# A graph layer on one core: 71 single rows a step in three register loads, one more filler, and the second block's gather places computed first

## The chip, the cores and the metric

The kernel runs on one core of a Trainium2 chip. The metric is the device time of one execution in microseconds (us), as the median of the runs; lower is better. The engines are named as the profile names them: PE multiplies matrices, PEld loads its weights, DVE is the vector engine, ACT the scalar engine, POOL issues the indirect gathers, SP is the sync engine. SP and ACT also issue direct DMAs; that work is not counted as busy time of an engine and shows as SPq and ACTq.

## The reference

There are 50,000 nodes with 128 numbers each, and 1,650,000 directed edges sorted by their destination. Every node has one edge to itself, and it is the last of the edges to that node.

```python
msg = where(edge_type == 0, x[src] @ W_data.T + b_data, x[src] @ W_control.T + b_control)
agg = segment_sum(msg, dst, 50000)
out = relu(agg + x @ W_self.T + b_self)
result = layernorm(x + out)          # over the 128 numbers of a node
```

## The kernel before

The kernel sums the rows of x first and multiplies by the weights once for each block of nodes.

**Blocks and steps.** The edge list is cut into NBLK blocks of Q = 2 steps. Block 0 and the last block are plain: they hold gathered edges alone, and the last one takes what is left. In every other block a step has 1,536 + F + S edges. R = 12 columns of 128 edges (SIZES) are fetched by 12 indirect gathers on POOL, so a full block has 24 gathers. S edges are single rows: each is fetched by a direct DMA of its own, 512 bytes, TURNS[0] of them from SP and TURNS[1] from ACT. F edges are fillers. Their rows come in place of self edges among the 1,536: a self edge need not be gathered, since the node's own column of x is added from x_t. `fill` puts the fillers' indices in the first F places of self edges that it finds in the step; if any step has fewer than F self edges among its 1,536, the program sets a flag in `find_bad` (through `loops`) and a second, general path runs. With the numbers before, F = 42 and S = 64, a block has 3,284 edges, NBLK is 503, and the last block has 13 gathers.

**Passes.** `gathers` issues 6 indirect gathers (PASS) for a tile y of which there are 10 (SLOTS); a tile is free again when PE has used it. So POOL can be 60 gathers ahead of PE. `products` multiplies each gathered column by a one-hot matrix `oh` of the destinations and adds it up in PSUM. In the last pass of a step the single rows come as one more product: PE first waits in `rows_fetched` until all the single rows of the block have landed.

**DVE.** For each block DVE computes the one-hot matrix of the block two ahead (`onehot`, `counts`, AHEAD = 2), and the gather indices of the block five ahead (`fill`, RAHEAD = 5), besides the sums, the moments and the normalised rows of earlier blocks (`add`, `begin_sums`, `moments`, `store`).

**Single rows.** `offsets` turns the source indices of a block into byte offsets on DVE, three blocks ahead. `single_rows(b, part)` loads a part of these offsets into registers, one load instruction (line 476) on SP and one on ACT, and then issues one DMA for each register (line 481). Before the change there are two parts of 32 registers on each engine. In the main loop the parts of block b + 2 stand in passes 0 and 1 of block b. Their tile `yx` has four buffers, so a buffer is free when PE is done with the block four before. On ACT the square root of every second block (`root`, line 583) stands behind the single rows, on SP the load of x's columns (`window`, line 421), the edge lists of the next ten blocks (`load_edges`, `spread_out`, `spread_in`) and the store of a block (`store_rows`, line 597). Each engine does what it has in the order of the program.

**Start.** Block 0's gathers need nothing but the first index tile. Block 1's gathers wait for `fill(1)`. Before the change DVE first does `positions(0)`, `onehot(0)` and `counts(0)`, and then `fill(1)`. PE has, ahead of its first product, the small products of `left_out_columns(1)` to `left_out_columns(4)`, each of which waits for that block's `fill`.

Of the kernel before, what the change touches and what calls it, by code (L numbers as in the profile page):

```python
# [37 lines left out]
PASS = 6  # L38
B = 112
C = R * Q  # L40
F = 42
TURNS = (32, 32)
S = sum(TURNS)
LOADS = 2
BEGIN = (0, -(-Q * TURNS[0] // 4) * 4)
X = BEGIN[1] + -(-Q * TURNS[1] // 4) * 4
R1 = R + 1
# [3 lines left out]
CE = Q * SIZE  # L51
BE = CE + Q * (F + S)
NBLK = 2 + (E - CE) // BE
# [33 lines left out]
def plain(b):  # L87

    return b == 0 or b >= NBLK - 1
# [6 lines left out]
def straight(ctx, tc, c, x, x_t, edges_t, edges_f, src_x, dst_first, first_p, out):  # L96
# [35 lines left out]
                   allow_small_or_imprecise_dtypes=True)  # L132
    FILL = Q * F + C1
    small = keep_ps.tile([P, 2 * W + F + 2 * FILL + 2], F32, name="small")
    num_ps, rank_no_ps = small[:, :2 * W], small[:, 2 * W:2 * W + F]
    lists = [small[:, 2 * W + F + i * FILL:][:, :FILL] for i in range(2)]
    sums_at = [small[:Q * F, 2 * W + F + 2 * FILL + i:][:, :1] for i in range(2)]

# [85 lines left out]
    def clear_sums():  # L224
        for t in sums:
            nc.vector.memset(t, 0.0)
            nc.vector.memset(t[0:3, 2, :], 1.0)
            nc.vector.memset(t[0:2, 2, :], 0.0)
# [122 lines left out]
    def left_out_columns(b):  # L351

        if not plain(b):
            pc = sums_at[b % 2]
            nc.tensor.matmul(pc, bys.pop(b).rearrange("p q f -> p (q f)"), ones_b[:, 0:1], start=True, stop=True)
            pcs[b] = pc

    def left_out_matrix(b):
        if not plain(b):
            z = fil.tile([Q * F, 2, P], BF16, name="z", bufs=RAHEAD + 1)  # L360
            at = fil.tile([Q * F, 1], F32, name="at")
            nc.vector.tensor_copy(at, pcs.pop(b))
            nc.vector.tensor_scalar(z.rearrange("p t n -> p (t n)"), node_no, at, None, op0=ALU.is_equal)
            zs[b] = z
# [44 lines left out]
    def window(b):  # L409
        if b % SPAN:  # L410
            return
        n = min(SPAN, NBLK - b)
        w = b // SPAN
        _, regs = nc.values_load_multi_w_load_instructions(
            base_i[0:1, w, :1 + n], engines=[SP], min_val=0, max_val=(N - B) * ROW,
            skip_runtime_bounds_check_because=CLAMPED)
        for i in range(n):
            bases[b + i] = regs[1 + i]
        at = nc.s_assert_within(regs[0], 0, (N - WIDE) * 4, skip_runtime_bounds_check_because=CLAMPED)
        xw = stp.tile([P, WIDE], F32, name="xw")  # L420
        nc.sync.dma_start(xw.bitcast(U8), x_t_bytes[:, bass.ds(at, 4 * WIDE)])
        wides[w] = xw

    def positions(b):

        _, regs = nc.values_load_multi_w_load_instructions(
            at_i[0:1, b, :], engines=[DVE], min_val=0, max_val=WIDE - B, skip_runtime_bounds_check_because=CLAMPED)
        tops = [B - W] * Q + [B, WIDE - B]
        places[b] = [nc.s_assert_within(r, 0, top, skip_runtime_bounds_check_because=CLAMPED)
                     for r, top in zip(regs, tops)]  # L430
        xT = stp.tile([P, B], F32, name="xT", bufs=5)
        nc.vector.tensor_copy(xT, wides[b // SPAN][:, bass.ds(places[b][3], B)])  # L432
        xTs[b] = xT

    def onehot(b):
        g, i = divmod(b, GB)
        oh = ohp.tile([P, C1, 2 * W], F32, name="oh")
        nc.vector.tensor_tensor(oh, col_g[g][:, i, :, None].to_broadcast([P, C1, 2 * W]),  # L438
                                num_ps[:, None, :].to_broadcast([P, C1, 2 * W]), op=ALU.is_equal)
        ohs[b] = oh  # L440

    def counts(b):

        cnt = ohp.tile([P, Q, 2 * W], BF16, name="cnt")
        with nc.allow_low_precision(reason="whole numbers up to R1"):
            nc.vector.tensor_reduce(cnt, ohs[b].rearrange("p (q r) w -> p q w r", r=R1), AX.X, ALU.add)  # L446
        cnts[b] = cnt
# [14 lines left out]

    def part_of(n, part):

        return min(n, 32 * part)

    def single_rows(b, part):

        if part == 0:
            ys[b] = stp.tile([S, Q, D], F32, name="yx", bufs=ROW_SLOTS)  # L470
        both = []
        for j, (eng, dma) in enumerate(((SP, nc.sync), (ACT, nc.scalar))):
            n = Q * TURNS[j]
            k0, k1 = part_of(n, part), part_of(n, part + 1)
            at = BEGIN[j]
            _, rows = nc.values_load_multi_w_load_instructions(ats[b][0:1, at + k0:at + k1], engines=[eng], **RANGE)
            both.append([(dma, fetched[j][b % ROW_SLOTS], *divmod(k0 + k, TURNS[j]), sum(TURNS[:j]), row)
                         for k, row in enumerate(rows)])
        for pair in zip_longest(*both):
            for dma, sem, q, k, at, row in filter(None, pair):  # L480
                copy = dma.dma_start(ys[b][at + k:at + k + 1, q, :].bitcast(U8), x_bytes[:, bass.ds(row, ROW)])
                copy.then_inc(sem, 16)
                tc.no_tile_sem_insts.add(copy.ins.name)
                tc.add_to_no_dep_group(f"single{b}", copy.ins)

    def rows_fetched(b):

        times = len(range(b % ROW_SLOTS or ROW_SLOTS, b + 1, ROW_SLOTS))
        for j in range(2):
            wait = nc.tensor.wait_ge(fetched[j][b % ROW_SLOTS], 16 * Q * TURNS[j] * times)  # L490
        tc.declare_fence(wait.ins, group=f"single{b}")
# [85 lines left out]
    def pair(b):  # L577

        return range(b // 2 * 2, b + 1) if b % 2 == 1 or b == NBLK - 1 else ()
# [55 lines left out]
    spread_out(0)  # L635
    spread_in(0)
    window(0)
    positions(0)
    onehot(0)
    counts(0)  # L640
    for b in range(1, RAHEAD):
        fill(b)
        left_out_columns(b)
        left_out_matrix(b)
        if b < AHEAD:
            onehot(b)
            counts(b)
            for part in range(LOADS):
                single_rows(b, part)
        if b == 1:  # L650
            clear_sums()
    ready = []
    for b in range(NBLK + 1):
# [20 lines left out]
        for q, (step, ks) in enumerate(passes_of(b)):  # L674
# [20 lines left out]
            if q == 1 and b > 1 and pair(b - 2):  # L695
                store(pair(b - 2))
                ready.extend(pair(b - 2))
            if q < LOADS and not plain(b + AHEAD):
                single_rows(b + AHEAD, q)
# [231 lines left out]
def gnn_resnorm(  # L931
# [46 lines left out]
    with ExitStack() as own:  # L978
        straight(own, tc, c, x, x_t, edges_t, edges_f, src_x, dst_first, first_p, out)
# [60 lines left out]
```

## Time and profile before

| | us |
|---|---|
| median of 3 runs | 15131.09 |
| lowest and highest run | 15127.51, 15135.05 |
| the profiled execution | 15137.27 |
| its span, first to last instruction | 15135.5 |
| POOL busy in it | 11419.4 (75%) |
| DVE busy in it | 10825.4 (72%) |
| PE busy in it | 7996.4 (53%) |

The span is 1.8 us shorter than the execution's own time. A timeline row has the start, the length, the engine, the line, what it does and how often, and in brackets how long the engine had been idle before and what ended that. Equal instructions of an engine that follow each other are merged in one row with their count: the length then goes from the start of the first to the end of the last. DMA issues on SP and ACT are such rows too. A row of a line (line 476, say) has the shortest, the median and the longest of its instructions in ns.

### The profile page before, as it was taken

What the parts mean: (1) busy time and instruction counts of PE and PEld (TensorE: products, weight loads), DVE (VectorE), ACT (ScalarE), POOL (GpSimd) and SP (SyncE); (2) the same over time, 40 slices, a digit from 0 to 9 for tenths busy, and PEclk for the clock granted to TensorE, in tenths of its full rate; (3) what the DMA queues carried; (4) which work ended last, traced back from release to release, by engine and by line L of the source; (5) the groups of instructions that cost most, each with busy time, mean ns of one, the idle gap of its engine ahead of it and who ended that gap; (6) DMA issues with size and microseconds to landing.
All of it is one profiled execution on the core that took longest, in us unless ns stands there. A gap on an engine that the chain in (4) does not pass through costs nothing. (4 is left out here: it accounts for less than half of the span.)

```text
span 15135.5 us, 239743 instructions
## 1 busy us (share of the span) xinstructions
PE 7996.4 (53%) x35339; PEld 6888.2 (46%) x35340; DVE 10825.4 (72%) x14081; ACT 77.8 (1%) x258; POOL 11419.4 (75%) x12071
## 2 busy tenths in 40 slices
PE   3555555555555555555555555555555555555555
PEld 3444444444444444444444444444444444444444
DVE  8777777776777777777777777777777777777775
ACT  0000000000000000000000000000000000000000
POOL 7777777777777777777777777777777777777777
PEclk7555555555555555555555555555555555555555
DMA  2222222222222222222222222222222222222222
GB/s 64 63 62 62 63 63 61 63 62 63 62 63 63 62 62 63 63 62 62 63 63 62 62 63 63 62 62 63 63 62 62 63 63 62 63 62 63 62 63 57
DMA packets 616955, 941.51 MB, mean 62 GB/s; under 512 B 272160, under 2 KB 409151, under 8 KB 615358
## 3 DMA queue, kind: packets, MB, share of 16 engines
q0 software_dynamic: 385968, 791.19, 21.8%
q1 hardware_dynamic: 164824, 118.13, 3.2%
q10 hardware_dynamic: 64566, 16.74, 0.8%
q14 instruction: 1309, 10.72, 0.2%
q8 instruction: 288, 4.72, 0.1%
HBM read 895.97 MB, written 29.02 MB: 61 GB/s over the span
## 5 line engine op out<-in xcount | busy, mean ns | idle before, releaser
L507 POOL DMA_INDIRECT y<-in_x,idx x12048 | 11405.6, 947 | 3690.8 <-issue 3598.2
L526 PE MATMUL acc<-oh,y 128*128 128x120 f32 x24122 | 5724.9, 426 | 6958.6 <-PEq L514 6911.9
L526 PEld LDWEIGHTS acc<-oh,y 128*128 128x128 f32 x24122 | 5178.2, 323 | 7419.1 <-PEq L514 7365.9
L540 DVE TENSOR_TENSOR sums<-acc,sums 128x180 f32 x1006 | 340.1, 338 | 3743.3 <-PE acc L535 3676.7
L446 DVE TENSOR_REDUCE cnt<-oh 128x240 bf16<-128x3120 f32 x503 | 2927.9, 5821 | 17.5
L438 DVE TENSOR_TENSOR oh<-col,small 128x3120 f32<-128x3120 f32 x503 | 1702.6, 3385 | 0.0
L348 DVE TENSOR_REDUCE by<-old 128x84 bf16<-128x1092 f32 x501 | 1067.5, 2131 | 17.4
L532 PE MATMUL acc<-oh,yx 64*128 64x120 f32 x2004 | 764.1, 482 | 0.0
L329 DVE TENSOR_TENSOR m<-rk,small 128x1092 f32<-128x1092 f32 x501 | 647.0, 1291 | 17.1
L332 DVE TENSOR_TENSOR new<-m,small 128x1092 f32<-128x1092 f32 x501 | 646.9, 1291 | 17.0
L336 DVE TENSOR_REDUCE v_new<-new 128x26 f32<-128x1092 f32 x501 | 646.6, 1291 | 17.0
L345 DVE TENSOR_TENSOR old<-m,small 128x1092 f32<-128x1092 f32 x501 | 642.8, 1283 | 0.0
L532 PEld LDWEIGHTS acc<-oh,yx 64*128 64x128 f32 x2004 | 488.6, 303 | 206.2 <-issue 200.0
L561 PE MATMUL po<-wmsgT,sums 128*112 128x128 f32 x2012 | 528.9, 409 | 0.0
L561 PEld LDWEIGHTS po<-wmsgT,sums 128*112 128x112 f32 x2012 | 384.6, 262 | 108.6 <-issue 89.7
L559 PE MATMUL po<-bias,sums 3*112 3x128 f32 x1006 | 341.7, 435 | 0.0
L558 PE MATMUL po<-wselfT,xT 128*112 128x128 f32 x1006 | 293.6, 391 | 0.0
L535 PE MATMUL acc<-cnt,to_row 128*128 128x60 bf16 x2012 | 278.1, 228 | 0.0
L551 DVE TENSOR_TENSOR sums<-pl,sums 128x336 f32<-128x336 f32 x501 | 254.0, 507 | 17.3
L558 PEld LDWEIGHTS po<-wselfT,xT 128*112 128x112 f32 x1006 | 257.4, 302 | 0.0
L559 PEld LDWEIGHTS po<-bias,sums 3*112 3x112 f32 x1006 | 197.8, 249 | 112.2 <-issue 96.6
L380 DVE TENSOR_TENSOR pl<-pl,xT 128x224 f32<-128x224 f32 x501 | 199.9, 399 | 53.5 <-DVE xT L432 2.1
(129 smaller groups left out, 3601.6 us busy)
## 6 DMA issues: line engine op xcount, KB each, us to landing
yx<-in_x ACTq DMA_DIRECT2D x32064, 0.5 KB
yx<-in_x SPq DMA_DIRECT2D x32064, 0.5 KB
y<-in_x,idx POOLq DMA_INDIRECT x12048
xw<-in_x_t SPq DMA_DIRECT2D x126, 224.0 KB
out<-o SPq DMA_DIRECT2D x503, 56.0 KB
vf_all<-vd SPq DMA_DIRECT2D x51, 420.0 KB
sdt<-in_edges_t SPq DMA_DIRECT2D x51, 390.0 KB
one_g<-in_src_x SPq DMA_DIRECT2D x51, 5.0 KB
```

Source lines behind the costliest of these rows:

```text
L329: nc.vector.tensor_tensor(m, rk_g[g][:, i, :, None].to_broadcast([P, C1, F]), rank_no_ps[:, None, :].to_broadcast([P, C1, F]), op=ALU.is_e ...
L332: nc.vector.tensor_tensor(new.rearrange("p (q r) f -> p q r f", r=R1), m.rearrange("p (q r) f -> p q r f", r=R1), vf.rearrange("p (q f) -> ...
L336: nc.vector.tensor_reduce(v, new, AX.X, ALU.add)
L345: nc.vector.tensor_tensor(old, m, cb[:, :, None].to_broadcast([P, C1, F]), op=ALU.mult)
L348: nc.vector.tensor_reduce(by, old.rearrange("p (q r) f -> p q f r", r=R1), AX.X, ALU.add)
L438: nc.vector.tensor_tensor(oh, col_g[g][:, i, :, None].to_broadcast([P, C1, 2 * W]), num_ps[:, None, :].to_broadcast([P, C1, 2 * W]), op=AL ...
L446: nc.vector.tensor_reduce(cnt, ohs[b].rearrange("p (q r) w -> p q w r", r=R1), AX.X, ALU.add)
L507: copy = nc.gpsimd.indirect_dma_start(out=y[:r, k % PASS, :].bitcast(U8), out_offset=None, in_=x_rows, in_offset=bass.IndirectOffsetOnAxis ...
L526: nc.tensor.matmul(acc[:, :2, :].rearrange("p t w -> p (t w)"), y[:r, k % PASS, :], ohs[b][:r, column(k), :], start=k == of_step[0], stop= ...
L532: nc.tensor.matmul(acc[:, :2, :].rearrange("p t w -> p (t w)"), ys[b][:, q, :], ohs[b][:S, q * R1 + R, :], start=False, stop=True)
L558: nc.tensor.matmul(po, xT, c["wselfT"], start=True, stop=False)
L561: nc.tensor.matmul(po, a[:, t, :B], c["wmsgT"][:, t * D:(t + 1) * D], start=False, stop=t == 1)
```

## The change

F goes from 42 to 43, TURNS from (32, 32) to (35, 36), so S from 64 to 71, and LOADS from 2 to 3. `part_of` cuts a block's rows on an engine into three parts at multiples of four: SP has 70 rows for a block, loaded as 24, 24 and 22 registers, and ACT has 72, loaded as 24, 24 and 24. The third part stands in pass 2. A full block then has 3,300 edges instead of 3,284, still with 24 gathers; NBLK becomes 501 instead of 503, and the last block is left with 228 edges, so 2 gathers. In the start, `positions(0)`, `onehot(0)` and `counts(0)` move behind `fill(1)` and what follows it for block 1.

```diff
-F = 42
-TURNS = (32, 32)
+F = 43
+TURNS = (35, 36)
 S = sum(TURNS)
-LOADS = 2
+LOADS = 3
...
     def part_of(n, part):
 
-        return min(n, 32 * part)
+        return -(-n * part // (4 * LOADS)) * 4 if part < LOADS else n
...
     window(0)
-    positions(0)
-    onehot(0)
-    counts(0)
     for b in range(1, RAHEAD):
         fill(b)
         left_out_columns(b)
         left_out_matrix(b)
+        if b == 1:
+            positions(0)
+            onehot(0)
+            counts(0)
         if b < AHEAD:
             onehot(b)
             counts(b)
```

## Prediction

> **What bounds the kernel now.** I read the page's costliest groups first, then the waits, then POOL's busy time in two long windows.
>
> ```profile
> L507 POOL DMA_INDIRECT y<-in_x,idx x12048 | 11405.6, 947 | 3690.8 <-issue 3598.2
> L526 PE MATMUL acc<-oh,y 128*128 128x120 f32 x24122 | 5724.9, 426 | 6958.6 <-PEq L514 6911.9
> L348 DVE TENSOR_REDUCE by<-old 128x84 bf16<-128x1092 f32 x501 | 1067.5, 2131 | 17.4
> L532 PE MATMUL acc<-oh,yx 64*128 64x120 f32 x2004 | 764.1, 482 | 0.0
> L329 DVE TENSOR_TENSOR m<-rk,small 128x1092 f32<-128x1092 f32 x501 | 647.0, 1291 | 17.1
> ```
>
> ```profile
> POOL y L507 <- issue: 3601.5, 11798, 0.3
> POOL y L507 <- PE acc L526: 28.5, 84, 3.2
> DVE sums L540 <- PE acc L535: 3676.7, 457, 14.3
> ```
>
> ```profile
> 3000.00:9000.00 6000.00, 4536.90 (x4794) 0.55 0.26 62
> 9000.00:15000.00 6000.00, 4536.22 (x4796) 0.53 0.26 62
> ```
>
> POOL is busy only 75% of the span, but its gaps are of one kind: 11,798 gaps of at most 0.3 us, put down to issue, which means that nothing the profile shows held it back. With 4,795 gathers in 6,000 us a gather comes every 1.2513 us, in both windows. PE's idle time is waiting in its queue (PEq) at line 514, which is the wait for gathered rows, and DVE's is waiting for PE. So the gathers set the pace: 24 of them give 30.03 us per block.
>
> **The gathers.** Before the last block there were 502 blocks of 24, so 12,048 gathers; now there are 500 of 24, 12,000. That is 48 x 1.2513 = 60.1 us less. The rest of the change only matters where it keeps POOL from this pace.
>
> **The end.** The last block drops from 13 gathers to 2.
>
> ```profile
> 15097.48 0.94 POOL L507 DMA_INDIRECT y<-in_x,idx  x1 [0.30 <-issue]
> ...
> 15105.03 0.35 DVE L540 TENSOR_TENSOR sums<-acc,sums 128x180 f32 x1
> ...
> 15118.80 0.76 PE L559 MATMUL po<-bias,sums 3*112 3x128 f32 x2
> ```
>
> The last full block's last gather starts at 15097.48, its sums are there at 15105.38. The products of its layer, which need these sums, run only at 15118.80, behind the passes of the last 13 gathers. With two gathers, which start 2.5 us after 15097.48, nothing stands between. 11 gathers are 13.8 us of POOL, and the layer can come 13.4 us earlier at most; a part of DVE's work on the last block gets in the way. I take 12.5 (bounds 0, if the tail were one fixed chain, and 13.8).
>
> **The start.** Here the change looks better than it is.
>
> ```profile
> 25.79 0.35 SPq L316 DMA_DIRECT2D vf_all<-vd  x1
> 27.14 0.38 SPq L421 DMA_DIRECT2D xw<-in_x_t  x1
> ```
>
> ```profile
> 31.40 0.22 DVE L432 COPY xT<-xw 128x112 f32 x1 [5.13 <-DMA xw<-in_x_t]
> ...
> 40.66 0.24 DVE L326 COPY small<-vf_all 128x84 f32<-128x84 f32 x1
> ```
>
> ```profile
> 45.80 0.94 POOL L507 DMA_INDIRECT y<-in_x,idx  x1 [9.52 <-DVE idx L340]
> ```
>
> ```profile
> 90.35 0.23 PE L355 MATMUL small<-ones_b,by 128*84 128x1 bf16 x1 [9.12 <-DVE by L348]
> ...
> 93.64 0.94 POOL L507 DMA_INDIRECT y<-in_x,idx  x1 [3.17 <-PE acc L526]
> ```
>
> POOL waits 9.52 us for block 1's indices, because `fill(1)` starts at 40.66 behind the one-hot work of block 0. Moved ahead, the indices come about 9 us earlier and this wait goes. What is late next is the row at 93.64: the 61st gather needs the first tile of ten back, and PE begins only after the small product at 90.35, which waits for the `fill` of block 4. Those fills lie at the end of the same DVE work, in another order. So POOL reaches gather 61 nine us earlier and waits there some 11 us instead of 3.17. What remains is a shorter start of DVE: it no longer waits for xw until 31.40 but for vf_all, which was issued 1.35 us earlier on the same queue; against it, four fills are longer by 26 of 1092 elements in each of five operations, (4 x 1.29 + 2.13) x 0.024 = 0.17 us each, 0.7 in all. When vf_all lands no row shows, only that it was there at 40.66. I take 0.7 us of gain, between a loss of 5 and a gain of 9.5 (if the slots did not bind).
>
> **Fillers and wider tiles elsewhere.** The 0.17 us per block on DVE lie under its 3676.7 us of waiting for PE, 7.3 us per block. A single-row product has 71 rows of weights instead of 64; one with 128 takes 426 ns and one with 64 takes 482, so rows cost nothing.
>
> **The single rows.** This is the part that can go wrong. SP and ACT issue the DMAs one by one, and both have more to do per block.
>
> ```profile
> 7523.21 10.36 ACTq L481 DMA_DIRECT2D yx<-in_x  x32
> ```
>
> ```profile
> 7523.21 23.51 ACTq L481 DMA_DIRECT2D yx<-in_x  x64
> 7555.61 0.29 ACT L583 ACTIVATE sd<-mv,eps 112x2 f32<-112x2 f32 x1 [60.67 <-DVE at L362]
> 7557.97 49.45 ACTq L481 DMA_DIRECT2D yx<-in_x  x128
> 7615.74 0.30 ACT L583 ACTIVATE sd<-mv,eps 112x2 f32<-112x2 f32 x1 [59.83 <-DVE at L362]
> ```
>
> ```profile
> L476 SPq TENSOR_LOAD <-at_x x799: 1864/2120/2358, 2999.3 to 14988.5; - x200
> L476 ACTq TENSOR_LOAD <-at_x x799: 2131/2233/2457, 3001.3 to 14983.1; - x200
> ```
>
> ```profile
> L980 ACTq TENSOR_LOAD <-bad x1: 463/463/463, 15125.4 to 15125.4; - x1
> ...
> L980 SPq TENSOR_LOAD <-bad x1: 482/482/482, 15130.0 to 15130.0; - x1
> ```
>
> On ACT, 32 DMAs take 10.36 us, so one every (10.36 - 0.23) / 31 = 0.327, a DMA's own 0.23 at the end. The difference between 128 and 64 rows, 49.45 - 23.51 = 25.94 us, is one block: two stretches of 10.36 and two load gaps of 2.61, of which the load is 2.23. Between the end of the second row and the square root at 7615.74 ACT is idle for 8 us in two blocks. A load of one register takes 0.463 and one of 32 takes 2.233: 0.057 per register and 0.41 fixed, so 1.78 for 24. The new block on ACT is three parts of 10.36 - 8 x 0.327 = 7.74 for the DMAs, 1.78 for the load and 0.38 of the gap around it: 29.7 us. By the four parts of the third row, (49.45 + 2.61) / 4 = 13.0 each, it is 29.9. I take 29.8, against 30.03 that the gathers take. So ACT fits, with 0.2 us left of 4.
>
> The Trainium skill, page "DMA: Bandwidth & Descriptors", section "Latency and other measured facts", puts a floor of about 600 ns under a register load. By that floor a load of 24 is 1.83 and the block on ACT an estimated 29.95 us, just under the gathers' pace; the trace's load of one register, at 0.463, is below the floor, so I keep 29.8.
>
> SP has 70 rows, and other work.
>
> ```profile
> 7530.75 23.29 SPq L481 DMA_DIRECT2D yx<-in_x  x64
> 7554.20 0.34 SPq L597 DMA_DIRECT2D out<-o  x1
> 7556.81 23.18 SPq L481 DMA_DIRECT2D yx<-in_x  x64
> ```
>
> From 7530.75 to 7556.81 is a block with its store and without waiting: 26.06. Six rows more are 2.0, six registers more 0.3, the third load's fixed part and gap 0.6: 29.0. A window every fourth block and the lists every tenth add about 0.5 on average, an estimate from the lengths of such rows (0.38, 0.35) and of a load. 29.5 is under 30.03 too.
>
> Neither margin has to hold in every block. The rows of a block are issued two blocks ahead, so ACT can fall some 55 us behind before PE waits, and PE some 60 us behind before POOL finds no free tile (60 gathers, 75 us, less the pass being worked on). Part of this reserve is used early:
>
> ```profile
> 501.38 41.45 ACTq L481 DMA_DIRECT2D yx<-in_x  x96
> ```
>
> Three parts take 41.45 us here, where they later take 49.45 - 12.97 = 36.5. If that is typical of the first 900 us, ACT loses 2 to 4 us a block there, 40 to 80 us, and wins it back at 0.2 us a block. I expect PE to lag POOL by tens of us in the first third, at no cost to POOL.
>
> **The sum.** 60.1 + 12.5 + 0.7 = 73.3 us less. The profiled execution took 15137.27 (span 15135.5 and 1.8 around it), so it would take 15064; the median of the runs is 6.2 below the profiled one, which gives 15058 us.
>
> **Rivals.**
>
> *ACT's queue becomes the bound (slower).* The mechanism: the third load costs more than its 24 registers suggest, or the DMAs come at 0.34 instead of 0.327, and a block on ACT takes longer than 30.03. For it speaks how thin the margin is; 0.013 us on each of 72 DMAs is 0.9 us a block. Against it, all loads and DMAs of the later windows are alike, and the sum by two rows is 29.7 and 29.9. If the block takes W, 499 blocks fall 499 x (W - 30.03) behind; the reserve of some 60 us takes the first 0.12. From W = 30.15 on the gain shrinks, and from 30.3 on it is gone. At 30.5 the cost is 235 - 60 = 175, so about 15230 us. The far end is a load of 24 that costs what one of 32 does, 2.23: then W is 31.2, the cost 520 and the time 15580.
>
> *It comes out even.* The same with W at 30.2 to 30.3, so 25 to 75 us of the 73 are lost: 15083 to 15133, most of it within 0.2% of before.
>
> *The start gives its full 9.5 us.* If PE's first products did not wait for the fills, POOL would gain the whole wait at 45.80: 15049. The row at 90.35 speaks against it.
>
> *The change doesn't do what it says.* With 43 fillers a step needs 43 self edges among its 1,536, or the general path runs, which would take far longer. The inputs decide this, not the trace: a count over the sorted edges finds the fewest in any step to be exactly 43, so it is enough.
>
> *Register loads priced per register.* At a price that made three loads of 24 dearer than the DMAs they feed, ACT would be bound in any case: with 0.2 us per register W is 3 x (7.74 + 4.8 + 0.38) = 38.8 us and the time about 19400. The 2.233 us for 32 registers are 0.07 each, so no chance is left for it. The Trainium skill states that figure, about 200 ns a register even in bulk, on the page "Runtime: NRT & Kernel Launch", section "Instruction fetch mechanics", for loads from HBM; the trace's loads, from a tile, do not follow it.
>
> **How the numbers follow.** The forecast has 0.68, the full start 0.03, ACT as the bound 0.20, the even case 0.09, the last two nothing. A change of 0.2% (30 us) is about what a measurement of this kernel can tell from none. Faster by more than that: 0.71; within it: 0.09; slower: 0.20. The forecast's own range is 15045 (full start, full tail) to 15085 (5 us lost at the start, no gain at the end, ACT slightly over). The range reaches on to 15165, through the even case and the beginning of the slower one.
>
> **What would show it.** Right: 12,002 gathers, still 1.251 us apart; ACT's square root hardly idle, with the rows of a block some 29.8 us apart; a register load of 24 at 1.78; DVE waiting for the square root in early blocks; at the start no wait of POOL for indices and one of about 11 us for the 61st gather. Wrong: POOL waiting for PE in hundreds of gathers with blocks more than 30.1 us apart and ACT never idle, a load of 24 above 1.9, or POOL's pitch itself longer than 1.2513.

## The result and the profile after

The changed kernel took 15452.74 us, the median of 6 runs (15449.53 to 15453.82). The kernel before took 15128.06 on the same chip (6 runs, 15124.21 to 15135.05). The ratio is 1.0213, with an interval of 1.02 to 1.0227: the change costs 2.1%. Forecast were 15058 and a range from 15045 to 15165. The profiled execution has a span of 15451.7 us; what follows is read from it.

The chain that ended last, on the page of the changed kernel, by engine and then by line:

```profile
ACTq 68%; issue 16%; DVE 12%; DMA 2%; PE 1%; POOL 1%; ACT 0%; SPq 0%; DVEq 0%; PEldq 0%; POOLq 0%
ACTq L481 56%; ACTq L476 12%; DVE cnt L446 3%; DVE oh L438 2%; DMA yx<-in_x 1%; DVE sums L540 1%; DVE o L592 1%; POOL y L507 1%; DVE m L329 1%; DVE new L332 1%; DVE v_new L336 1%; DVE old L345 0%; PE acc L526 0%; ACT sd L583 0%; DVE rstd L589 0%
```

More than two thirds of the span go through ACT's queue: the row DMAs of line 481 and their register loads of line 476. The gathers on POOL, which set the pace before, have 1%. The waits and the costliest groups of the changed kernel say the same:

```profile
ACT sd L583 <- issue: 15071.0, 246, 63.5
PE acc L532 <- PEq L490: 4535.9, 448, 21.9
POOL y L507 <- issue: 3503.9, 11477, 0.3
DVE rstd L589 <- ACT sd L583: 2635.5, 246, 12.4
POOL y L507 <- PE acc L526: 234.5, 127, 10.9
POOL y L507 <- PE acc L532: 197.4, 31, 10.6
```

```profile
L507 POOL DMA_INDIRECT y<-in_x,idx x12000 | 11333.9, 944 | 4049.1 <-issue 3503.3 <-PE acc L526 234.5 <-PE acc L532 197.4
L532 PE MATMUL acc<-oh,yx 71*128 71x120 f32 x1996 | 584.0, 386 | 4536.1 <-PEq L490 4535.9
L348 DVE TENSOR_REDUCE by<-old 128x86 bf16<-128x1118 f32 x499 | 1083.4, 2171 | 17.2
```

PE now waits at line 490, for single rows, 448 times in 499 blocks; before, the idle time ahead of the row product was 0.0. ACT's square root, once in two blocks, stands behind nothing but rows: 15071.0 / 246 = 61.26 us of idle time and 0.29 of its own make 61.55 us for two blocks, 30.78 for one. The gathers need 30.03, so POOL now waits for PE. Its busy time fell by 71.7 us and its idle time rose by 358.3 (4049.1 against 3690.8).

POOL's busy time in the two windows of the changed kernel:

```profile
3000.00:9000.00 6000.00, 4411.13 (x4673) 0.61 0.29 61
9000.00:15000.00 6000.00, 4408.35 (x4670) 0.61 0.29 61
```

A gather now comes every 1.284 us instead of 1.2513.

Why ACT's block got longer is not in the loads. The register loads of the changed kernel from 3 to 15 ms, and two blocks of ACT's queue:

```profile
L476 ACTq TENSOR_LOAD <-at_x x1168: 1658/1774/2038, 3007.5 to 14999.9; - x195
```

```profile
12000.97 59.91 ACTq L481 DMA_DIRECT2D yx<-in_x  x144
12060.98 0.29 ACT L583 ACTIVATE sd<-mv,eps 112x2 f32<-112x2 f32 x1 [61.62 <-issue]
```

The load of 24 takes 1.774, as forecast. ACT issues 144 rows in 59.91 us with no pause but the loads, and within a part its DMAs are 0.349 us apart on average, not 0.327. What lengthens them shows where a block of rows ends. The timeline of the changed kernel:

```profile
7994.25 60.54 ACTq L481 DMA_DIRECT2D yx<-in_x  x144
8028.04 28.30 SPq L481 DMA_DIRECT2D yx<-in_x  x70
8054.89 0.29 ACT L583 ACTIVATE sd<-mv,eps 112x2 f32<-112x2 f32 x1 [62.24 <-issue]
8069.57 0.79 PE L532 MATMUL acc<-oh,yx 71*128 71x120 f32 x2 [6.21 <-PEq L490]
```

ACT issued the last row of a block at 8054.8, SP at 8056.3. PE, which was idle for 6.21 us and waits for nothing else, gets that block only at 8069.57. So the rows are under way for more than ten us after their issue. In the chain there are such pieces:

```profile
430.03 11.79 DMA yx<-in_x
```

The packet records of the trace give the number of rows that wait: the row DMAs that an engine has issued, less the 512-byte packets of its queue that have started, with those of the stores taken out. In the changed kernel mostly 23 to 31 rows wait in SP's queue and as many in ACT's, from 0.4 ms to the end, seldom more than 32, and a row's packet starts 11.7 us after its issue. The kernel before was like that from about 0.3 to 0.9 ms (mostly 19 to 32 waiting, 12 us); from 1.5 ms on mostly 0 to 7 rows waited, and 1.1 us passed. "Full" below means a queue in which some 28 rows wait like that. Where the queues are full, the issue itself takes longer: a row DMA keeps ACT 0.272 us on average from 0.4 to 0.9 ms of the kernel before and 0.239 from 1.2 ms on, and 0.256 in the changed kernel. So ACT is held back by the rows' own pace.

Section 3 of the two pages, the queues with their packets, megabytes and share (q1 is SP's, q10 ACT's), first of before, then of the changed kernel:

```profile
q10 hardware_dynamic: 64566, 16.74, 0.8%
```

```profile
q10 hardware_dynamic: 72294, 18.74, 1.4%
```

12% more packets take about 1.8 times as long.

### The profile page after: what moved, and what is told of

Read it like the earlier page. It is cut to its first block, busy times and chain, and to the rows that moved or that the text cites. A ratio compares the mean times of both kernels' runs of the same rounds, so it can differ in the third digit from the quotient of the medians.

```text
span 15451.7 us, 253703 instructions
## 1 busy us (share of the span) xinstructions
PE 6391.4 (41%) x35177; PEld 5786.4 (37%) x35178; DVE 10889.6 (70%) x14029; ACT 77.3 (1%) x257; POOL 11337.3 (73%) x12012
## 3 DMA queue, kind: packets, MB, share of 16 engines
q0 software_dynamic: 384080, 787.32, 23.1%
## 4 chain that ended last, share of the span: by engine, by line
ACTq 68%; issue 16%; DVE 12%; DMA 2%; PE 1%; POOL 1%; ACT 0%; SPq 0%; DVEq 0%; PEldq 0%; POOLq 0%
ACTq L481 56%; ACTq L476 12%; DVE cnt L446 3%; DVE oh L438 2%; DMA yx<-in_x 1%; DVE sums L540 1%; DVE o L592 1%; POOL y L507 1%; DVE m L329 1%; DVE new L332 1%; DVE v_new L336 1%; DVE old L345 0%; PE acc L526 0%; ACT sd L583 0%; DVE rstd L589 0%
## 5 line engine op out<-in xcount | busy, mean ns | idle before, releaser
L507 POOL DMA_INDIRECT y<-in_x,idx x12000 | 11333.9, 944 | 4049.1 <-issue 3503.3
L526 PEld LDWEIGHTS acc<-oh,y 128*128 128x128 f32 x24004 | 4136.6, 268 | 3793.5 <-PEq L514 3780.3
L526 PE MATMUL acc<-oh,y 128*128 128x120 f32 x24004 | 4407.3, 359 | 125.2 <-PEq L514 125.1
L532 PE MATMUL acc<-oh,yx 71*128 71x120 f32 x1996 | 584.0, 386 | 4536.1 <-PEq L490 4535.9
L532 PEld LDWEIGHTS acc<-oh,yx 71*128 71x128 f32 x1996 | 410.7, 257 | 4660.0 <-PEq L490 4659.3
L348 DVE TENSOR_REDUCE by<-old 128x86 bf16<-128x1118 f32 x499 | 1083.4, 2171 | 17.2
L332 DVE TENSOR_TENSOR new<-m,small 128x1118 f32<-128x1118 f32 x499 | 658.8, 1320 | 17.1
L329 DVE TENSOR_TENSOR m<-rk,small 128x1118 f32<-128x1118 f32 x499 | 658.8, 1320 | 16.9
L336 DVE TENSOR_REDUCE v_new<-new 128x26 f32<-128x1118 f32 x499 | 657.7, 1318 | 17.0
L345 DVE TENSOR_TENSOR old<-m,small 128x1118 f32<-128x1118 f32 x499 | 654.9, 1312 | 0.0
L535 PEld LDWEIGHTS <-to_row 128*128 128x128 bf16 x2002 | 263.9, 132 | 27.8
```

Source lines behind the costliest of these rows:

```text
L329: nc.vector.tensor_tensor(m, rk_g[g][:, i, :, None].to_broadcast([P, C1, F]), rank_no_ps[:, None, :].to_broadcast([P, C1, F]), op=ALU.is_e ...
L332: nc.vector.tensor_tensor(new.rearrange("p (q r) f -> p q r f", r=R1), m.rearrange("p (q r) f -> p q r f", r=R1), vf.rearrange("p (q f) -> ...
L336: nc.vector.tensor_reduce(v, new, AX.X, ALU.add)
L348: nc.vector.tensor_reduce(by, old.rearrange("p (q r) f -> p q f r", r=R1), AX.X, ALU.add)
L507: copy = nc.gpsimd.indirect_dma_start(out=y[:r, k % PASS, :].bitcast(U8), out_offset=None, in_=x_rows, in_offset=bass.IndirectOffsetOnAxis ...
L526: nc.tensor.matmul(acc[:, :2, :].rearrange("p t w -> p (t w)"), y[:r, k % PASS, :], ohs[b][:r, column(k), :], start=k == of_step[0], stop= ...
```

## The experiments

"Needed" below means the rows of a block over the gathers' 30.03 us; "served" the rows of a block over the length of ACT's block while the queues are full.

**69 rows.**

```diff
-TURNS = (35, 36)
+TURNS = (34, 35)
```

> 69 single rows a step (34 SP, 35 ACT) in place of 71, all else as in the changed kernel; 12,018 gathers. Theory A (the single rows of both queues are served at one shared rate; in the changed kernel 142 rows in 30.85 us, 0.217 us each, with some 25 to 30 rows waiting in each queue): 138 rows need 29.98 us, just under the 30.03 us of the gathers, so the backlog of the start is hardly worked off but POOL keeps its pace: 15070 to 15130 us. Theory B (each queue serves its own rows, ACT at 0.4285 us each): 70 rows on ACT need 30.0 us, the same as A. Theory C (issuing on ACT costs 30.85 us for 72 rows, nothing waits behind it): two rows and two registers less on ACT are 0.8 us, so 30.05 us, about 15090 us. All three are close here; the queues' depth in the trace tells more than the time.

15420.09 us, ratio 1.0193 (1.0178 to 1.0209). All the theories missed. The queues stay full to the end (18 to 31 rows in ACT's). ACT's block, from its square roots as above, is 30.71 us; 138 / 30.71 = 4.49 rows a us, less than the 4.61 with 71 rows. So a fixed time for each row, theory A's form, is not exact: 138 rows take nearly as long as 142.

**67 rows.**

```diff
-TURNS = (35, 36)
+TURNS = (33, 34)
```

> 67 single rows a step (33 SP, 34 ACT); 12,032 gathers, 29 fewer than before, 36 us. Theory A: 134 rows need 29.1 us, under 30.03, so the backlog goes and the time is that of the gathers: about 15092 us, faster than before by 0.25%, and the rows wait 1 to 3 us from issue to their packet as before the change. Theory B: 68 rows on ACT at 0.4285 are 29.1 us, the same. Theory C: 29.3 us, the same time, with an issue every 0.34 us as in the changed kernel.

15090.76 us against 15126.29, ratio 0.9977 (0.9968 to 0.9986): faster than the kernel before by 0.23%, and the best version found. The timeline of this kernel early on, and POOL's busy time on the gathers in two windows:

```profile
1515.13 0.29 ACT L583 ACTIVATE sd<-mv,eps 112x2 f32<-112x2 f32 x1 [61.25 <-DVE small L326]
1517.02 56.60 ACTq L481 DMA_DIRECT2D yx<-in_x  x136
1573.72 0.29 ACT L583 ACTIVATE sd<-mv,eps 112x2 f32<-112x2 f32 x1 [58.29 <-issue]
```

```profile
3000.00:9000.00 6000.00, 4535.35 (x4798) 0.54 0.25 62
9000.00:15000.00 6000.00, 4535.74 (x4797) 0.54 0.24 62
```

Early, two blocks take 58.6 us with ACT never idle, and the queues are full; the mean block of that stretch is 29.57 us, 4.53 rows a us served, 4.46 needed. The small difference empties the queues slowly: a row's wait begins to fall at 2.4 ms and is back at about 1.2 us by 4.2 ms. ACT's blocks are shorter than the gathers' all that time, and POOL has its pace of 1.2507 us to the end (the windows, of the gathers).

**20 rows on SP, 36 on ACT.**

```diff
-TURNS = (35, 36)
+TURNS = (20, 36)
```

> 56 single rows a step, 20 on SP and 36 on ACT: ACT has exactly what it has in the changed kernel (72 rows, three loads of 24), SP 40 rows in place of 70; 12,113 gathers, 52 more than before, 65 us. Theory A (shared service): 112 rows need 24.3 us, no backlog, ACT issues every 0.327 us, a block on ACT takes 29.8 us as predicted, and the time is that of the gathers: about 15195 us. Theory B (ACT's own queue) and theory C (ACT's issuing): ACT takes 30.85 us a block as in the changed kernel, 503 blocks, so about 15540 to 15570 us.

36302.11 us in all. With 56 single rows the steps are cut at other edges, and one of them has 42 self edges, fewer than its 43 fillers. So the general path ran after the straight one, and only the straight part, up to about 15185 us, can be read. Its gathers and ACT's square roots:

```profile
1000.00:5000.00 4000.00, 3023.67 (x3200) 0.62 0.23 62
5000.00:9000.00 4000.00, 3024.18 (x3199) 0.62 0.23 62
9000.00:15000.00 6000.00, 4529.48 (x4792) 0.62 0.23 62
```

```profile
ACT sd L583 <- issue: 14893.7, 249, 60.5
```

ACT has 72 rows in three loads, as in the changed kernel, and its block takes (14893.7 / 249 + 0.29) / 2 = 30.05 us; 0 to 5 rows wait in ACT's queue, and POOL has its 1.250 us (1.252 in the last window). Those 30.05 us are a shade over the gathers' 24 x 1.250 = 30.0, and PE does wait 912.2 us for rows in the whole run, which POOL hardly feels. So neither the issuing nor a limit of ACT's own queue makes 30.8 (theories B and C fall). It needs SP's rows beside them.

**Each row as two halves.** 

```diff
-                copy = dma.dma_start(ys[b][at + k:at + k + 1, q, :].bitcast(U8), x_bytes[:, bass.ds(row, ROW)])
+                copy = dma.dma_start(ys[b][at + k:at + k + 1, q, :].bitcast(U8).rearrange("o (h e) -> o h e", h=2),
+                                     x_bytes[:, bass.ds(row, ROW)].rearrange("o (h e) -> o h e", h=2))
```

> The changed kernel with each single row copied as two runs of 256 bytes in one DMA instead of one run of 512; the number of DMAs is the same. Theory A with one DMA engine as the server and its time given by bytes: two engines share the work if the two runs go to two engines, the backlog goes, about 15060 us. Theory A with a cost per DMA or per packet on the server: no gain, 15450 us or slower (up to twice the service time, 60 us a block, if both runs go through the same engine one after the other). Theory C (issuing alone): 15450 us, unless an issue with two runs itself takes longer.

15469.01 us, ratio 1.0226 (1.0211 to 1.0242). The packets in the trace still have 512 bytes, one for each row, so the two halves were one run again when they were moved. It is a repeat of the changed kernel and says nothing on the bytes.

**The kernel before with 28 rows on SP and 36 on ACT.**

```diff
-TURNS = (32, 32)
+TURNS = (28, 36)
-LOADS = 2
+LOADS = 3
...
-        return min(n, 32 * part)
+        return -(-n * part // (4 * LOADS)) * 4 if part < LOADS else n
```

> The kernel before with 28 row DMAs per step on SP and 36 on ACT (TURNS = (28, 36)), three register loads, 42 fillers: 64 rows per step and the same blocks as before, while ACT has as many rows as in the changed kernel. Theory A (both queues share one service of about 4.4 to 4.6 rows a us; it is the sum of 142 rows per block that is too much): 128 rows need 4.26 a us, the rows queue only in the first part as before, ACT's blocks then take 30.1 us, and the time is 15128 to 15200. Theory B (ACT's queue has a limit of its own, some 0.4285 us per row): 72 rows take 30.85 us per block and the time is about 15500.

15130.58 us, ratio 0.9999 (0.9985 to 1.0013); rows, blocks and gathers are those of the kernel before. The row product of this kernel:

```profile
L532 PE MATMUL acc<-oh,yx 64*128 64x120 f32 x2004 | 768.0, 484 | 1.8 <-PEq L490 1.8
```

PE waits 1.8 us for rows in the whole run. The same 72 rows of ACT cost nothing when SP has 56 in a block instead of 70. Theory A stands in this point, though the early full queues that it expected did not come (a row's median wait is 1.06 us over the whole run), and B falls a second time.

**32 and 32 rows, the rest of the change kept.**

```diff
-TURNS = (35, 36)
+TURNS = (32, 32)
```

> The changed kernel with 32 and 32 rows per step instead of 35 and 36; everything else of the change stays: 43 fillers, three register loads (parts of 24, 20 and 20 rows), the second block's places first. 12,054 gathers at 1.2513 us. Theory A: the rows keep up, 15100 to 15130: the fillers, the third load and the new start cost nothing. Rival (the third load or the longer fills carry the loss): 15300 or more.

15118.14 us, ratio 0.9992 (0.9977 to 1.0006). The third load, the 43 fillers and the new start lose nothing; the whole loss is in the seven more rows a step.

**Gathers of 64 rows.** Each gather and its product take at most 64 of their 128 rows; the rest of the sums is left out. The same edit stands in two places, at the gather and at its product.

```diff
-            r = REST_ROWS[k] if b == NBLK - 1 else SIZES[k % R]
+            r = min(64, REST_ROWS[k] if b == NBLK - 1 else SIZES[k % R])
```

> The changed kernel with each gather and its product cut to at most 64 of its 128 rows (the other rows are left out of the sums); the single rows are as in the changed kernel. What serves the single rows: if it is a limit of their own (A1, about 4.6 rows a us whatever else moves), the rows still queue, a block takes 30.85 us and the time stays at 15430 to 15460. If the single rows lose their time to the gathers' packets on the same DMA engines (A2), half of these packets are gone, the row queues stay nearly empty, and a block is bound by ACT's issuing at 30.1 us or by POOL: 15000 to 15120.

15406.01 us, ratio 1.018 (1.0166 to 1.0195). The waits and the queues of this kernel:

```profile
ACT sd L583 <- issue: 11283.2, 185, 64.4
PE acc L532 <- PEq L490: 4903.1, 484, 16.5
```

```profile
q0 software_dynamic: 384064, 394.05, 11.1%
q10 hardware_dynamic: 72294, 18.74, 2.3%
```

The gathers move half the bytes, in as many packets, and yet PE waits for rows 484 times. ACT's block is (11283.2 / 185 + 0.29) / 2 = 30.64 us, so 4.63 rows a us are served, as in the changed kernel. So the rows do not lose their time to the gathers' bytes. The text of A2 speaks of the gathers' packets, and says that half of them are gone; their number stayed (384,064 against 384,080), so a share of the rows' time that goes to the number of those packets was not tested. A1 is near (its 30.85 and its 15430 to 15460 are missed by 0.2 us and 24 us).

**34 and 34 rows, 42 fillers.**

```diff
-F = 43
-TURNS = (35, 36)
+F = 42
+TURNS = (34, 34)
```

> The changed kernel with 34 and 34 rows per step and 42 fillers: 136 rows per block and 12,032 gathers, so the gathers alone would make 15092. 136 rows per 30.03 us are 4.53 a us. Theory A puts the service at 4.4 to 4.6 with a queue, so this is its threshold: 15090 to 15150 if the queues of the first part drain, 15380 to 15400 if the rows stay queued to the end. Theory that the load of three parts carries the loss: as with 67 rows, 15092.

15196.4 us, ratio 1.0042 (1.0028 to 1.0056), between the two cases. The square roots and the gathers of this kernel:

```profile
ACT sd L583 <- issue: 12580.2, 209, 62.0
```

```profile
3000.00:9000.00 6000.00, 4527.19 (x4783) 0.61 0.28 62
9000.00:15000.00 6000.00, 4504.77 (x4762) 0.61 0.28 62
```

The queues stay full (23 to 31 rows in ACT's). A block is (12580.2 / 209 + 0.29) / 2 = 30.24 us, 4.50 rows a us, where 4.53 are needed. That little is lost in every block: 500 x 0.21 = 105 us, and 15196 is 104 above the 15092 that the gathers alone would make. POOL keeps its pace until it has used up its free tiles, and then falls to 1.260 us per gather.

Put together:

| single rows of a step | needed a us | served a us, queues full | the queues | us |
|---|---|---|---|---|
| 64 (before) | 4.26 | 4.49 (128 / 28.53, 0.31 to 0.60 ms) | empty by 1.5 ms | 15128 |
| 67, 43 fillers | 4.46 | 4.53 (1.0 to 2.4 ms) | empty by 4.2 ms | 15091 |
| 68, 42 fillers | 4.53 | 4.50 | full to the end | 15196 |
| 69, 43 fillers | 4.60 | 4.49 | full to the end | 15420 |
| 71, 43 fillers (the change) | 4.73 | 4.61 | full to the end | 15453 |

Where the rows needed stay below the rows served, the queues empty and the gathers set the time; where they do not, the rows set it. The rate served is not one constant: from 68 to 69 rows ACT's block grows by 0.47 us, from 69 to 71 by 0.07.

**Queues kept short.** One question was left: are 4.5 to 4.6 rows a us all that the chip gives, or does it give more while the queues are short? The traces hint at more. In stretches of 5 us away from stores, in which SP and ACT issue at least 5.8 rows a us together, the packet records show about 5.1 served with the kernel before, 5.2 with 67 rows and 5.5 with 64 rows in three loads, all with short queues; with both queues full it is 4.6 to 4.9 (67 rows early, 68, 69, 71). To test it, SP and ACT wait until their earlier rows have landed: before each part, or at blocks 60 and 120 alone; with 71 rows, and with the 34 and 34 rows and 42 fillers above.

```diff
+            if True:                               # or: part == 0 and b in (60, 120)
+                a = b if part else b - 1
+                if not plain(a):
+                    times = len(range(a % ROW_SLOTS or ROW_SLOTS, a + 1, ROW_SLOTS))
+                    dma.wait_ge(fetched[j][a % ROW_SLOTS], 16 * (n * (times - 1) + (k0 if part else n)))
```

> The changed kernel (71 rows), in which SP and ACT, before the first row DMA of each part and after its register load, wait until all row DMAs of their earlier parts have landed; so no queue ever holds more than one part of 24. Theory of two states (the rows are served at some 4.5 a us only while about 30 wait in each queue; with the queues nearly empty they are served at least as fast as SP and ACT issue together, 2 / 0.327 = 6.1 a us): the load of 1.78 us covers the landing, ACT's block takes 30.1 to 30.4 us, and the time is 15060 to 15180. Theory of one fixed rate (142 rows per block at 4.6 a us whatever the queue holds): the block takes 30.85 us or, with the waits, more: 15440 to 15600.

> The changed kernel with that wait at the start of two blocks alone, 60 and 120 (near 1.8 and 3.7 ms). Two states, each of which lasts once entered: from then on the queues stay nearly empty and POOL is back at 1.251 us per gather, 15070 to 15130. Fixed rate, or a state that fills again by itself at 71 rows: the queues are full again some blocks later, 15430 to 15460.

> 34 and 34 rows (the kernel that took 15196) with the wait at blocks 60 and 120 alone. Two states: 136 rows per 30.03 us are 4.53 a us, which the fast state carries as it does 134; the queues stay nearly empty after the wait, 15090 to 15110. Fixed rate: 15190 to 15200 as without it.

> 34 and 34 rows with the wait before each part. Two states: 15088 to 15105, POOL at its pace throughout. Fixed rate: 15190 or more.

These four ran on another chip, on which the kernel before takes 23172 us. All four ran there again (kernel before 23633), and two of them a third time (23135).

| kernel | us | ratio to before | again | ratio | a third time | ratio |
|---|---|---|---|---|---|---|
| 71, wait each part | 23952 | 1.0335 (1.0318 to 1.0352) | 24211 | 1.0251 (1.0228 to 1.0274) | 23937 | 1.0336 (1.0315 to 1.0357) |
| 71, wait at two blocks | 23937 | 1.0328 (1.0311 to 1.0345) | 24241 | 1.0263 (1.024 to 1.0286) | - | - |
| 68, wait at two blocks | 23676 | 1.0216 (1.0199 to 1.0233) | 24012 | 1.0162 (1.0139 to 1.0185) | 23663 | 1.0222 (1.0202 to 1.0242) |
| 68, wait each part | 23664 | 1.0211 (1.0194 to 1.0228) | 24032 | 1.0171 (1.0149 to 1.0194) | - | - |

> 71 rows, SP and ACT wait before each part until the rows of their earlier parts have landed. Two states (some 4.5 rows a us with about 30 waiting in each queue, 6.1 a us with the queues nearly empty): ACT's block 30.1 to 30.4 us, 15060 to 15180. One fixed rate of 4.6 a us: 15440 to 15600. On a chip whose kernel before takes over 20000 us it says nothing.

> 68 rows (15196 without a wait), the wait at blocks 60 and 120 alone. Two lasting states: 136 rows per 30.03 us stay in the fast state, 15090 to 15110. Fixed rate: 15190 to 15200. On a chip whose kernel before takes over 20000 us it says nothing.

The timeline of 71 rows with the wait at two blocks says why they answer nothing:

```profile
8026.10 0.29 ACT L588 ACTIVATE sd<-mv,eps 112x2 f32<-112x2 f32 x1 [94.53 <-DVE at L362]
8027.98 88.96 ACTq L486 DMA_DIRECT2D yx<-in_x  x144
```

144 rows take ACT 88.96 us here, against 59.91 on the first chip, while seldom more than 3 rows wait in its queue. SP and ACT themselves are slow: in some stretches each of their instructions takes some 0.7 us. The rows never queue, so whether a short queue is served faster was not tested. It stays open.

## Why the prediction was wrong

**The failed step: "So ACT fits, with 0.2 us left of 4."** ACT's block was put at 29.8 us from rows of a stretch in which the queues were empty, and a DMA was taken to cost its issue alone. Two things were wrong in it. The smaller: with 72 rows and short queues the block takes 30.05 (the run with 20 and 36), so 0.25 were missing already and the margin was nothing. The prediction took 0.327 us a DMA from one row of the timeline; the mean within a part is 0.334 in the kernel before from 1.2 ms on, and 0.341 in that run. (Its second sum, from 13.0 us a part, comes to 29.8 and not 29.9; nothing hangs on it.) The larger: the rows of SP and ACT share a service behind the issue. It gives 4.5 to 4.6 rows a us with full queues, and the change asks for 142 / 30.03 = 4.73. The sum had no term for it. That term is 30.78 - 30.05 = 0.73 us a block.

**The misread row: 501.38.** The three parts in 41.45 us were in sight, and the prediction read them as an early loss, of which it says that ACT "wins it back at 0.2 us a block". They were the same full queues, and that stretch had the limit in it. Two of its square roots, in the timeline of the kernel before:

```profile
313.89 0.30 ACT L583 ACTIVATE sd<-mv,eps 112x2 f32<-112x2 f32 x1 [51.77 <-issue]
599.18 0.30 ACT L583 ACTIVATE sd<-mv,eps 112x2 f32<-112x2 f32 x1 [55.95 <-issue]
```

They are ten blocks apart, and ACT loads and issues without a pause between them: 28.53 us for 128 rows are 4.49 a us, below the 4.73 that 142 rows need. At that rate 142 rows take 31.6 us, which is the loss.

**The rival that came true.** "ACT's queue becomes the bound (slower)", with a chance of 0.20, is what happened, by the second of its two ways (it named 0.34 us for a DMA, and the mean in the changed kernel is 0.351), not by the dearer load. Its price holds roughly: W of 30.78 gives 499 x 0.75 = 374 us. With the 60 us of reserve that is 15372, without it 15432; measured were 15453. The reserve saved nothing. Its part on ACT was never there: in the changed kernel ACT issues the last row of block 6 at 216.1 us and PE's first product with that block's rows starts at 230.9: a lead of 15 us, not of some 55. In the kernel before the lead is 22 us at block 6 and 60 at block 51; it grew while ACT's blocks, at 28.5 us, were shorter than the gathers'. In the changed kernel they never are. The part on POOL was used (45 us ahead of PE at block 51), but the last rows end the kernel, not the last gathers. From ACT's first row at 20.5 us to its last at 15419.7 a block takes 30.86 us, and 32 us more end the span.

**What was right.** The gathers: 12,000 and 2, and 1.251 us apart where nothing holds them (67 rows). The load of 24: 1.774 against 1.78. The fills: 1291 to 1320 ns for four operations and 2131 to 2171 for the fifth make 0.16 us for a block, against 0.17. The row product with 71 rows: 386 ns, no dearer than 482, but at another granted TensorE clock (0.615 against 0.543 before), so the two do not show the price of a row. The start, in the changed kernel's timeline:

```profile
92.25 0.94 POOL L507 DMA_INDIRECT y<-in_x,idx  x1 [10.89 <-PE acc L526]
```

The wait for indices is 1.2 us instead of 9.52, and the 61st gather waits 10.89, as forecast ("some 11"); it starts 1.4 us earlier than before, against 0.7. The end term of 12.5 can't be read, since the last rows now set the end. The flag for too few self edges stayed off, and it came on with 56 rows, where a step has 42.

**The rule that was not weighed.** In the packet records, rows of both queues are served one after another: away from stores, a packet of the two row queues begins more than 0.012 us before the end of the one ahead of it in 3% of the cases in the changed kernel, and in 0.1% of those of the kernel before from 3 ms on. And of the 16 data packets of a gather, about one is slow when the queues are full: 0.83 per gather take over 0.6 us (mean 0.99; the median packet takes 0.23), against 0.35 per gather in the steady part of before.

The Trainium skill, page "DMA: Bandwidth & Descriptors", says in "Queues, rings and completion order" that SP's and ACT's DMAs run on the same 16 engines and that each of these serves its queues in turn, a packet at a time. The same page of the Trainium skill says in "Why a DMA increments its semaphore by 16 and not by 1" that such a copy runs on up to 16 engines, how many depends on its sizes, and that they are the lowest-numbered ones. In the trace a row is one packet of 512 bytes, so it is not spread over several engines. By the page all the single rows of SP and ACT would then be on one engine, together with its sixteenth of every gather. The two observations agree with that; which engine a packet runs on is not in the trace, so no run here shows it, and why the rate is 4.5 to 4.6 rows a us stays open. The rule would have spoken against the change.

## What to carry to other kernels

A DMA issued from a queue had two prices here, the issue (one every 0.33 us on each of SP and ACT) and the service behind it (4.5 to 4.6 rows a us), and the two queues shared the second: divide the DMAs of a stage by its time, and look for a stretch in which the queue was full, since only there the trace shows the limit. A slow stretch early in a trace that goes away by itself can be such a measurement, as it was here. Near the limit a few per cent decide: 67 rows here gain 0.23%, 68 lose 0.4%, because with 68 the queue never empties and costs 0.21 us in each of 500 blocks.

## What was not expected of the hardware

- Single 512-byte rows from SP and ACT together are served at 4.5 to 4.6 a us with full queues; some 28 wait in each, a row then starts 12 us after its issue instead of 1.1, and the issuing engine is slowed to that pace.
- Halving the bytes of the gathers (787 to 394 MB) left that rate as it was (4.61 and 4.63).
- 69 rows are served slower (4.49) than 71 (4.61). No run explains it.
- With products of 64 rows the granted TensorE clock was 1.0, with those of 128 rows 0.615, at nearly the same time (15404.4 and 15451.7 us of span).
- On another chip the same kernel before took 23172 us, with SP's and ACT's instructions at some 0.7 us each in places.
